# Softmax maxima and sums of a quantized cross-attention: maxima from the scores in PSUM, sums by products over transposed exponentials

## The chip, the cores and the metric

The kernel runs on one core of a Trainium2 chip. The metric is the device time of one execution in microseconds. Of the kernel before, eight runs are known: median 4922.11, from 4911.96 to 4927.17. One more execution was profiled; every duration and every instant below is from its trace, instants counted from the start of its span.

A core has five engines with a queue of instructions each: TensorE (PE, whose weight loads are shown as PEld), VectorE (DVE), ScalarE (ACT), GpSimd (POOL) and SyncE (SP, which here only issues transfers). Every engine works through its queue in order; semaphores tie them together.

## The reference, cut to what matters

The network is four blocks one after another on x (4 x 1024 tokens of 288 numbers) with a context of 4 x 64 tokens. The change is in the third block, a transformer block whose attention is "fake quantized": queries, keys and values are rounded to 256 levels over the whole tensor, and so are the probabilities, whose step is the largest probability of the whole tensor divided by 255. Its cross-attention, with 16 heads of 18 numbers:

```python
def _quant_attention(x, ctx, Wq, Wk, Wv, Wo, bo):
    q = (x @ Wq).reshape(bsz, sq, H, HD).transpose(0, 2, 1, 3)
    k = (ctx @ Wk).reshape(bsz, sk, H, HD).transpose(0, 2, 1, 3)
    v = (ctx @ Wv).reshape(bsz, sk, H, HD).transpose(0, 2, 1, 3)
    q = _fake_quant(q, NBITS)
    k = _fake_quant(k, NBITS)
    v = _fake_quant(v, NBITS)
    scale = 1.0 / np.sqrt(HD).astype(np.float32)
    scores = jnp.einsum('bhqd,bhkd->bhqk', q, k) * scale
    probs = jax.nn.softmax(scores, axis=-1)
    probs = _fake_quant(probs, SMBITS, always_zero=True)
    out = jnp.einsum('bhqk,bhkd->bhqd', probs, v)
```

Since the step of the probabilities is known only when the largest of all of them is, the kernel goes over the scores twice. The **first pass** finds, for every token and head, the largest exponential and the sum of the 64 exponentials; the largest quotient of the two over the tensor gives the step. The **second pass** computes the exponentials again, rounds them to levels and multiplies them by the values.

## The kernel before, in words

The function is `fq_tail`. Its first half, under `with (self.psum8("f2"), ...)` in line 3274, is the first pass; the rest is the second pass together with the block's feed-forward stage. P is 128, H 16 heads, T 64 context tokens, NG 4 groups of four heads, HP 32 (a head's 18 numbers padded to 32), and NT 32 tiles of 128 tokens, eight for each of the four samples b.

For each of the 32 tiles t the first pass does this:

- **Rounding** on VectorE: two operations in `fq_levels` (L818, L819) and a third (L3302) turn the tile's queries `qn` into integer levels, written in bf16 to one of three padded tiles `pads`.
- **Transposes** on TensorE (L3308, four of 128x128 into one PSUM bank), copied by ScalarE to `qT` (L3312) and written by a transfer of SP to a scratch tensor `qb` (L3313), from which the second pass reads.
- **Scores** on TensorE (L3318): four products, one for each group of heads, with `qT` as the weights and 256 columns of `kbd4` (four heads by 64 keys, block diagonal), into two PSUM banks. Tokens are on the partitions, head and key along the row.
- **Exponentials** on ScalarE (L3325), two of 128x512, into `e` (f32). The scale is read from a register, `rstep`.
- **Maxima** on VectorE (L3331): the largest of the 64 exponentials of each head, to `top`.
- **Sums** of the 64: two halvings by additions on GpSimd (L3333, 512 a row, and L3335, 256 a row), and the last 16 on VectorE (L3336), to `sums`.

PSUM is eight buffers of one bank (`psum8`), used in turn. The work tiles have three buffers each.

Behind the loop stands `prob_shift` (L2475), a chain mostly on VectorE over all 32 x 16 values of a partition: the reciprocal of the sums (L2483), its product with `top`, the largest over all partitions (L825 and a reduction over partitions on GpSimd), a logarithm (L838), and three bf16 `parts` (L2493). When it is done, the pools of the first pass are given back, and SP issues the feed-forward weights (`w`, L2517) and then the first `qT` of the second pass (L3362).

The order of the instructions in the queues is not that of the source: a scheduler in the language's compiler moves them within the dependencies, such as the roundings of later tiles ahead of the maxima of earlier ones. The function that prepares the next block's weights, `self_aside`, is spread through the stage as well; its reductions over weights (L1581 and L1582, on VectorE) stand among the last tiles of the first pass.

Of the kernel before, what the change touches and what calls it, by code (L numbers as in the profile page):

```python
# [28 lines left out]
F32 = mybir.dt.float32  # L29
BF16 = mybir.dt.bfloat16  # L30
I32 = mybir.dt.int32
AF = mybir.ActivationFunctionType
ALU = mybir.AluOpType
AX = mybir.AxisListType
PSUM = bass.MemoryType.PSUM

P = 128
B, S, C, H, D, T, FF = 4, 1024, 288, 16, 18, 64, 1152
NTB = S // P
NT = B * NTB  # L40
CK, NC3 = 96, 3
HP = 32
NG = 4
# [1136 lines left out]
class Fast(Net):  # L1180
# [2080 lines left out]
    def fq_tail(self, w, kq, keep, rawq, mx, nmn, beside):  # L3261
# [4 lines left out]
        tc, nc = self.tc, self.nc  # L3266
        with ExitStack() as es:
# [4 lines left out]
            kt = {k: gp.tile(keep[k][1], BF16, name=k) for k in ("kbd", "vbd")}  # L3272
            qb = [dr.tile([P, NG, S], BF16, name=f"qb{b}") for b in range(B)]
            with (
                self.psum8("f2"),
                tc.tile_pool(name="f2q", bufs=1) as qp,
                self.work("f2k0", 3),
            ):
                kt["kbd4"] = qp.tile(keep["kbd4"][1], BF16, name="kbd4")
                for k, (d, _) in keep.items():  # L3280
                    nc.sync.dma_start(kt[k], d)
                top = qp.tile([P, NT, H], F32, name="top")
                sums = qp.tile([P, NT, H], F32, name="sums")
                qn = qp.tile([P, NT, C], F32, name="qn")
                for b in range(B):
                    nc.sync.dma_start(qn[:, b * NTB : (b + 1) * NTB, :], rawq[b])
                pads = [qp.tile([P, H, HP], BF16, name=f"pads{n}") for n in range(3)]
                for pd in pads:
                    nc.gpsimd.memset(pd, 0.0)
                q = self.global_params(gp, mx, nmn, "qq")  # L3290
                self.watch_range(-0.5, 255.5, q["zp"], "qzext")
                step = gp.tile([P, 1], F32, name="step")
                nc.vector.tensor_scalar(
                    step, q["d"], kq["d"][:, 0:1], SCALE, ALU.mult, ALU.mult
                )
                rstep = self.scale_register("cstep", step)

                for t in range(NT):
                    b, j = divmod(t, NTB)
                    pd = pads[t % 3]  # L3300
                    self.fq_levels(qn[:, t, :], q, 0)
                    nc.vector.tensor_scalar(  # L3302
                        pd[:, :, :D], self.heads(qn[:, t, :]), q["top"], None, ALU.min
                    )
                    ps = self.ps1(BF16)
                    pf = pd.rearrange("p h d -> p (h d)")
                    for g in range(NG):
                        nc.tensor.transpose(  # L3308
                            ps[:, g * P : (g + 1) * P], pf[:, g * P : (g + 1) * P], self.idb
                        )  # L3310
                    qT = self.wk.tile([P, NG, P], BF16, tag="qT1", name="qT1")
                    nc.scalar.copy(qT, ps[:, : NG * P].rearrange("p (g t) -> p g t", t=P))  # L3312
                    nc.sync.dma_start(qb[b][:, :, j * P : (j + 1) * P], qT)  # L3313
                    e = self.wk.tile([P, H, T], F32, tag="e1", name="e1")
                    for m in range(2):
                        ps = self.ps1()
                        for g in (2 * m, 2 * m + 1):
                            nc.tensor.matmul(  # L3318
                                ps[:, (g % 2) * 256 : (g % 2 + 1) * 256],
                                lhsT=qT[:, g, :],  # L3320
                                rhs=kt["kbd4"][:, b, g, :],
                                start=True,
                                stop=True,
                            )
                        nc.scalar.activation(  # L3325
                            e[:, 8 * m : 8 * m + 8, :],
                            ps.rearrange("p (h k) -> p h k", k=T),
                            AF.Exp,
                            scale=rstep,
                        )  # L3330
                    nc.vector.tensor_reduce(top[:, t, :], e, AX.X, ALU.max)  # L3331
                    e2 = self.wk.tile([P, H, T // 2], F32, tag="e2", name="e2")
                    nc.gpsimd.tensor_tensor(e2, e[:, :, : T // 2], e[:, :, T // 2 :], ALU.add)  # L3333
                    e4 = self.wk.tile([P, H, T // 4], F32, tag="e4", name="e4")
                    nc.gpsimd.tensor_tensor(e4, e2[:, :, : T // 4], e2[:, :, T // 4 :], ALU.add)  # L3335
                    nc.vector.tensor_reduce(sums[:, t, :], e4, AX.X, ALU.add)  # L3336
                pd, parts = self.prob_shift(gp, qp, top, sums, step)
            pv = gp.tile([P, 1], F32, name="pv")
            nc.vector.tensor_tensor(pv, pd, kq["d"][:, 1:2], ALU.mult)
# [304 lines left out]
```

## Time and profile before

| what | us |
|---|---|
| median of eight runs | 4922.11 |
| the profiled execution, its time | 4919.14 |
| its span, first to last instruction | 4917.3 |
| busy in the span: PE, PEld | 4237.8, 1704.6 |
| busy in the span: DVE, ACT, POOL | 3004.4, 3067.5, 1263.3 |
| mean granted TensorE clock (1 is full) | 0.853 |
| first pass over the context, first rounding to last sum | 2936.0 to 3041.7 |
| `prob_shift`, to its last part | 3041.7 to 3058.4 |
| `w` and the first `qT` landing, first addition of the second pass | 3077.9 |

The profiled execution lies 3.0 us below the median of the runs. In a line of groups the columns are: source line, engine, operation, output and input by the program's names with their shapes and the number of instructions; then their busy time in us and the mean duration in ns; then the idle time of the engine just before them and what ended it. In a line of the timeline: start in us, duration in us, engine, line, operation. A duration is longer than the distance to the next start where instructions of one engine overlap. In a line by stretches: the stretch, its length, the busy time of each engine with the number of its instructions, the mean granted TensorE clock, the share of the transfer engines and GB/s.

### The profile page before, as it was taken

The numbers are of one execution on the slowest core, as the hardware profiler recorded it, in microseconds if no ns is written. First come the engines' busy times: TensorE is split into PE (matmuls) and PEld (weight loads), VectorE is DVE, ScalarE is ACT, GpSimd is POOL, SyncE is SP. The second block draws the span as 40 slices with busy tenths as digits, with TensorE's granted clock in tenths as the row PEclk, the third lists the DMA queues.
The fourth block names the chain that finished last, engine by engine and source line by source line (L and its number), as shares of the span: only waits on it lengthen the run. The fifth ranks groups of instructions, "written<-read, shape, count | busy, mean of one in ns | idle before, by whom it ended". The sixth has DMA issues, their size and how long they took to land. (4 is left out here: it accounts for less than half of the span.)

```text
span 4917.3 us, 63638 instructions
## 1 busy us (share of the span) xinstructions
PE 4237.8 (86%) x23227; PEld 1704.6 (35%) x23227; DVE 3004.4 (61%) x6707; ACT 3067.5 (62%) x4347; POOL 1263.3 (26%) x1900
## 2 busy tenths in 40 slices
PE   4999998888998979998788863899998999998776
PEld 2223223445565411110233331455443223222343
DVE  8355445755654589999788878333234355445775
ACT  3776775664753279998888853212113776775796
POOL 2001001543222576410112225111111001003664
PEclk9999999889999955555788885899998999998897
DMA  3000002100001221000010022101000000001000
GB/s 85 3 5 21 14 8 74 41 31 7 13 13 55 112 63 33 26 7 0 22 28 25 23 93 70 32 9 34 1 3 17 2 4 29 7 12 38 12 17 21
DMA packets 137700, 135.98 MB, mean 28 GB/s; under 512 B 69276, under 2 KB 114972, under 8 KB 135712
## 3 DMA queue, kind: packets, MB, share of 16 engines
q1 hardware_dynamic: 136176, 128.13, 8.6%
q0 software_dynamic: 1200, 3.69, 0.3%
q8 instruction: 184, 3.01, 0.3%
q14 instruction: 140, 1.15, 0.1%
HBM read 79.92 MB, written 43.47 MB: 25 GB/s over the span
## 5 line engine op out<-in xcount | busy, mean ns | idle before, releaser
L2082 ACT ACTIVATE e<-ps 128x1024 f32<-128x1024 f32 x1024 | 992.6, 1021 | 406.9 <-PE ps L2072 399.5
L2072 PE MATMUL ps<-qT,kT 32*128 32x512 f32 x4096 | 622.4, 647 | 2.0 <-DVE sext L1994 2.0
L3110 DVE TENSOR_REDUCE top<-e 128x2 f32<-128x2048 f32 x256 | 563.6, 2280 | 14.8 <-ACT e L3103 14.6
L2028 PE MATMUL ps<-e,v 128*32 128x512 f32 x4096 | 555.0, 613 | 8.5 <-DVE oT L2039 8.5
L3479 PE MATMUL ps<-qk 32*128 32x512 bf16 x1024 | 499.9, 604 | 40.7 <-ACT e L3103 38.8
L3528 ACT ACTIVATE e<-ps 128x1024 f32<-128x1024 f32 x512 | 484.0, 1053 | 76.8 <-PE ps L3519 59.2
L3103 ACT ACTIVATE e<-ps 128x1024 f32<-128x1024 f32 x512 | 520.5, 1153 | 6.8 <-PE ps L3479 3.7
L1807 POOL TENSOR_TENSOR x<-x,y 128x288 f32<-128x288 f32 x192 | 153.5, 808 | 787.8 <-DVE y L1806 482.2
L3531 DVE TENSOR_SCALAR eb<-e 128x2048 bf16<-128x2048 f32 x256 | 322.0, 1261 | 47.1 <-ACT e L3528 44.6
L3519 PE MATMUL ps<-qk,kz 64*128 64x512 bf16 x1024 | 224.6, 436 | 48.0 <-ACT e L3528 46.2
L2546 PE MATMUL psf<-hT,w 128*128 128x512 f32 x576 | 257.9, 600 | 0.6 <-ACT hT L2538 0.6
L2072 PEld LDWEIGHTS ps<-qT,kT 32*128 32x128 f32 x4096 | 183.6, 184 | 201.0 <-issue 127.7
L1427 POOL TENSOR_TENSOR h<-h,g 128x288 f32<-128x288 f32 x160 | 130.8, 819 | 426.0 <-ACT h L1424 416.1
L2028 PEld LDWEIGHTS ps<-e,v 128*32 128x32 f32 x4096 | 81.3, 108 | 403.1 <-issue 344.4
L3479 PEld LDWEIGHTS <-qk 32*128 32x128 bf16 x1024 | 53.0, 99 | 465.1 <-issue 464.2
L3428 ACT ACTIVATE gl<-psf,bf 128x512 f32<-128x512 f32 x72 | 46.0, 684 | 269.5 <-PE psf L2550 265.1
L1356 ACT COPY qT<-ps 128x640 bf16<-128x640 bf16 (+3 forms) x252 | 149.7, 640 | 76.8 <-PE ps L1351 76.6
L1924 POOL TENSOR_TENSOR v<-y,wv1b 128x288 f32<-128x288 f32 x64 | 51.7, 814 | 559.1 <-DVE y L1921 559.1
L1351 PE MATMUL ps<-idb,q 128*128 128x128 bf16 (+2 forms) x1128 | 110.7, 243 | 91.1 <-ACT q L1335 60.9
L3432 DVE SCALAR_TENSOR_TENSOR u<-psf,bf,gl 128x512 f32<-128x512 f32 x72 | 51.2, 746 | 218.5 <-ACT gl L3428 218.5
L278 PEld LDWEIGHTS <-qT 98*128 98x128 bf16 (+2 forms) x1344 | 135.5, 105 | 120.8 <-issue 49.3
L3103 ACT ACTIVATION_READ_ACCUMULATOR e<-ps 128x1 f32 x512 | 172.9, 338 | 0.0
(509 smaller groups left out, 7755.4 us busy)
## 6 DMA issues: line engine op xcount, KB each, us to landing
raw<-y SPq DMA_DIRECT2D x32, 432.0 KB
in<-raw SPq DMA_DIRECT2D x30, 432.0 KB
kz<-qk SPq DMA_DIRECT2D x128, 64.0 KB
wn<-in_L_wfc SPq DMA_DIRECT2D x12, 432.0 KB
x<-in_x SPq DMA_DIRECT2D x4, 1152.0 KB
vvo<-vt SPq DMA_DIRECT2D x16, 288.0 KB
vo<-vvo SPq DMA_DIRECT2D x4, 1152.0 KB
rawq<-y SPq DMA_DIRECT2D x32, 144.0 KB
```

Source lines behind the costliest of these rows:

```text
L1356: nc.scalar.copy(qT[:, c0 : c0 + r, j0 * P : (j0 + per) * P].rearrange("p c (a t) -> p a c t", a=per), ps[:width, : per * r * P].rearrange ...
L1807: nc.gpsimd.tensor_tensor(self.x[:, t, :], self.x[:, t, :], y, ALU.add)
L2028: nc.tensor.matmul(acc[i * HP : (i + 1) * HP, :], lhsT=st["v"][:, kt, h * (D + 1) : h * (D + 1) + HP], rhs=es_[i // 2][:, i % 2, :], start ...
L2072: nc.tensor.matmul(pss[i // 2][:, i % 2, :], lhsT=self.row_tile(kT, i)[:, kt * P : (kt + 1) * P], rhs=self.row_tile(qT, i)[:, qh * 512 : ( ...
L2082: nc.scalar.activation(e, ps, AF.Exp, scale=SCALE)
L2546: nc.tensor.matmul(o, lhsT=lhs(i)[:, c, :], rhs=rhs(i)[:, c, :], start=(c == 0), stop=False)
L3103: nc.scalar.activation(e[:, j, :].rearrange("p (a n) -> p a n", a=2), sc, AF.Exp, scale=rstep, accum_out=sums[:, t, h0 + j : h0 + j + 1],)
L3110: nc.vector.tensor_reduce(top[:, t, h0 : h0 + 2], e, AX.X, ALU.max)
L3479: self.last = self.nc.tensor.matmul(ps[:, c, :], lhsT=self.row_tile(qT, i)[:, g, qt * P : (qt + 1) * P], rhs=self.row_tile(kT, i)[:, g, c ...
L3519: nc.tensor.matmul(pss[i][:, n, :], lhsT=kz[rows, i, kt * P : (kt + 1) * P], rhs=qT[rows, g, qh * 512 : (qh + 1) * 512], start=True, stop= ...
L3528: nc.scalar.activation(e[:, 2 * n : 2 * n + 2, :], ps, AF.Exp, scale=step)
L3531: nc.vector.tensor_scalar(eb, e, MAGIC, MAGIC, ALU.add, ALU.subtract)
```

## The change

The first pass is written anew for four tiles at a time (a set; there are eight).

For each tile, `largest` does the rounding, the transposes, the copy to `qT` (now a part of a 512-token tile for the set) and the four score products as before. The scores go to one buffer of two PSUM banks, and VectorE takes the maximum of the scores straight from PSUM. The exponential of all the maxima is taken once, after the loop (`top`, 128x512).

For each set, `total` computes the scores a second time the other way round, with keys on the partitions and 512 tokens along the row: for each group of heads a pair of 64-row bf16 products (`kbd`) into two banks, and one exponential of 128x1024 into `e`. Then eight f32 products with `pick`, a matrix of zeros and ones, add up the 64 rows of each head; each gives 32 rows of one bank, `acc`, so that four of them fill it, and the second four add to the first. ScalarE copies `acc` to `sT`, four small f32 products with `back` (16 columns) turn it back to tokens on the partitions, and VectorE copies 128x64 of it to `sums`.

`total` is a generator with a step after each exponential, one after `sT` and its end; a step of each running `total` is taken after each `largest`. So the sums of a set are worked out among the next two sets' tiles, and those of the last set after the loop.

PSUM goes from eight buffers of one bank to three of two banks (`ps2`) and two of one (`ps1`). The additions on GpSimd are gone.

```diff
-                self.psum8("f2"),
+                self.psum_attn("f2"),
...
-                for t in range(NT):
+                pick = qp.tile([P, 2, HP], F32, name="pick")
+                nc.gpsimd.memset(pick, 0.0)
+                for k in range(4):
+                    rows = slice(k % 2 * 64, (k % 2 + 1) * 64)
+                    nc.gpsimd.memset(pick[rows, k // 2, k : k + 1], 1.0)
+                back = qp.tile([P, H], F32, name="back")
+                nc.gpsimd.tensor_copy(
+                    back.rearrange("p (g i) -> p g i", i=4),
+                    self.idf.rearrange("p (g k) -> p g k", k=HP)[:, :, :4],
+                )
+
+                def largest(t, qT):
...
-                    qT = self.wk.tile([P, NG, P], BF16, tag="qT1", name="qT1")
                     nc.scalar.copy(qT, ps[:, : NG * P].rearrange("p (g t) -> p g t", t=P))
                     nc.sync.dma_start(qb[b][:, :, j * P : (j + 1) * P], qT)
-                    e = self.wk.tile([P, H, T], F32, tag="e1", name="e1")
-                    for m in range(2):
-                        ps = self.ps1()
-                        for g in (2 * m, 2 * m + 1):
+                    ps = self.ps2()
+                    for g in range(NG):
+                        nc.tensor.matmul(
+                            ps[:, g // 2, g % 2 * 256 : (g % 2 + 1) * 256],
+                            lhsT=qT[:, g, :],
+                            rhs=kt["kbd4"][:, b, g, :],
+                            start=True,
+                            stop=True,
+                        )
+                    nc.vector.tensor_reduce(
+                        top[:, t, :], ps.rearrange("p a (h k) -> p (a h) k", k=T), AX.X, ALU.max
+                    )
+
+                def total(n, qT):
+
+                    es_ = []
+                    for g in range(NG):
+                        ps = self.ps2()
+                        for pr in range(2):
+                            rows = slice(pr * 64, (pr + 1) * 64)
                             nc.tensor.matmul(
-                                ps[:, (g % 2) * 256 : (g % 2 + 1) * 256],
-                                lhsT=qT[:, g, :],
-                                rhs=kt["kbd4"][:, b, g, :],
-                                start=True,
-                                stop=True,
+                                ps[:, pr, :], lhsT=kt["kbd"][rows, n // 2, g, :],
+                                rhs=qT[rows, g, :], start=True, stop=True,
                             )
-                        nc.scalar.activation(
-                            e[:, 8 * m : 8 * m + 8, :],
-                            ps.rearrange("p (h k) -> p h k", k=T),
-                            AF.Exp,
-                            scale=rstep,
+                        e = self.wk.tile([P, 2, 512], F32, tag="e1", name="e1", bufs=6)
+                        nc.scalar.activation(e, ps, AF.Exp, scale=rstep)
+                        es_.append(e)
+                        yield
+                    acc = self.ps1()
+                    for pr in range(2):
+                        for g in range(NG):
+                            nc.tensor.matmul(
+                                acc[g * HP : (g + 1) * HP, :], lhsT=pick[:, pr, :],
+                                rhs=es_[g][:, pr, :], start=(pr == 0), stop=(pr == 1),
+                            )
+                    sT = self.wk.tile([P, 512], F32, tag="sT", name="sT")
+                    nc.scalar.copy(sT, acc)
+                    yield
+                    ps = self.ps1()
+                    for j in range(4):
+                        nc.tensor.matmul(
+                            ps[:, j * H : (j + 1) * H], lhsT=sT[:, j * P : (j + 1) * P],
+                            rhs=back, start=True, stop=True,
                         )
-                    nc.vector.tensor_reduce(top[:, t, :], e, AX.X, ALU.max)
-                    e2 = self.wk.tile([P, H, T // 2], F32, tag="e2", name="e2")
-                    nc.gpsimd.tensor_tensor(e2, e[:, :, : T // 2], e[:, :, T // 2 :], ALU.add)
-                    e4 = self.wk.tile([P, H, T // 4], F32, tag="e4", name="e4")
-                    nc.gpsimd.tensor_tensor(e4, e2[:, :, : T // 4], e2[:, :, T // 4 :], ALU.add)
-                    nc.vector.tensor_reduce(sums[:, t, :], e4, AX.X, ALU.add)
+                    nc.vector.tensor_copy(
+                        sums[:, 4 * n : 4 * n + 4, :].rearrange("p t h -> p (t h)"),
+                        ps[:, : 4 * H],
+                    )
+
+                running = []
+                for n in range(NT // 4):
+                    qT = self.wk.tile([P, NG, 512], BF16, tag="qT1", name="qT1")
+                    for j in range(4):
+                        largest(4 * n + j, qT[:, :, j * P : (j + 1) * P])
+                        running = [t for t in running if next(t, running) is not running]
+                    running.append(total(n, qT))
+                while running:
+                    running = [t for t in running if next(t, running) is not running]
+                nc.scalar.activation(top, top, AF.Exp, scale=rstep)
                 pd, parts = self.prob_shift(gp, qp, top, sums, step)
```

## The prediction

> **What bounds it now.** The chain of waits is no help: it holds one 0.8 us step, since it follows a branch at the end of the kernel. So I read the granted clock and the engines by stretches, then the groups of the stretch that the change touches, then its timeline. The stretches, columns PE, PEld, DVE, ACT and POOL busy, PEclk, DMA share, GB/s:
>
> ```profile
> 2350.00:2363.00 13.00, 8.62 (x68) 3.21 (x67) 9.49 (x10) 12.64 (x15) 1.39 (x2) 1.00 0.09 21
> 2364.00:2370.00 6.00, 5.38 (x27) 0.97 (x25) 4.55 (x4) 5.98 (x8) 0.00 (x0) 0.50 0.00 0
> 2936.00:3041.70 105.70, 49.66 (x256) 27.57 (x256) 95.14 (x178) 53.05 (x97) 64.34 (x64) 0.50 0.26 66
> 3041.70:3058.50 16.80, 0.00 (x0) 0.00 (x0) 16.37 (x50) 2.54 (x3) 0.38 (x1) 0.50 0.01 1
> ```
>
> The third line is the first pass over the context: 105.7 us, DVE busy for 95, no other engine for 65, the clock at half throughout. The fourth is the chain on DVE behind it (`prob_shift`), which starts once all sums are there. So the pass is DVE's, and what it loses is read from its groups:
>
> ```profile
> L3333 POOL TENSOR_TENSOR e<-e 128x512 f32<-128x512 f32 x32 | 40.5, 1267 | 39.2 <-ACT e L3325 30.4 <-ACT qT L3312 8.5
> L3331 DVE TENSOR_REDUCE top<-e 128x16 f32<-128x1024 f32 x32 | 38.7, 1208 | 3.1 <-ACT e L3325 3.0
> L819 DVE TENSOR_SCALAR qn<-qn,qqnzp 128x288 f32<-128x288 f32 x32 | 19.1, 598 | 0.0
> L818 DVE TENSOR_SCALAR qn<-qn,qqrd 128x288 f32<-128x288 f32 x32 | 15.6, 497 | 0.0
> L3336 DVE TENSOR_REDUCE sums<-e 128x16 f32<-128x256 f32 x32 | 13.0, 408 | 7.5 <-POOL e L3335 7.5
> ```
>
> L819 takes 598 ns in the mean, but its median is 365. The timeline shows why:
>
> ```profile
> 2984.81 1.26 POOL L3333 TENSOR_TENSOR e<-e 128x512 f32<-128x512 f32 x1 [0.25 <-ACT e L3325]
> 2984.94 1.30 DVE L819 TENSOR_SCALAR qn<-qn,qqnzp 128x288 f32<-128x288 f32 x1
> 2986.15 0.73 POOL L3335 TENSOR_TENSOR e<-e 128x256 f32<-128x256 f32 x1
> 2986.16 0.89 DVE L818 TENSOR_SCALAR qn<-qn,qqrd 128x288 f32<-128x288 f32 x1
> 2986.97 1.21 DVE L3331 TENSOR_REDUCE top<-e 128x16 f32<-128x1024 f32 x1
> 2988.10 0.40 DVE L3336 TENSOR_REDUCE sums<-e 128x16 f32<-128x256 f32 x1
> ```
>
> A rounding on DVE that starts inside a POOL addition ends with it, whatever its own 0.36 us; the reduction does not mind (1.21). From L3302 at 2979.72 to L3302 at 2998.58 six tiles pass, 3.14 us each. Of that, start to start, the maximum is 1.13, the sum 0.33, three roundings 3 x 0.28 = 0.84; the other 0.84 is DVE held behind POOL or waiting.
>
> **What the change removes and adds on DVE.** Gone are 32 sums (0.33), all POOL work (64.5 us) and with it the 0.84. Kept are the roundings, 0.84, and the maximum, now over two PSUM banks. No row reduces from PSUM. The nearest pair: a 128x512 reduction from SBUF takes 686 ns (L1219), a 128x512 copy out of PSUM 690 (L3395), so I take 1.13; bounds 1.13 and 1.20. [...] New is one copy of 128x64 out of PSUM for four tiles, about 0.16 (64 elements at the reduction's 1.1 ns, and 0.09). A set of four tiles thus costs DVE 4 x (0.84 + 1.13) + 0.16 = 8.04 us, where it took 12.56.
>
> **On ACT**, a set: four qT copies (589 ns, 0.54 start to start), four exponentials of 128x1024 (1.02, as L3103), one copy of the sums' 128x512 (0.59): 6.9 us, against 4 x (0.54 + 1.08) = 6.5. Under DVE's 8.04, so only its order matters.
>
> **On PE**, a set had 16 transposes and 16 products of 256 columns (0.63 and 1.03 us per four at half clock). Added: (S) four pairs of 64-row bf16 products; a pair lies side by side (two L3376 start 0.1 us apart, the third 0.4 later, at half clock), so 0.43 a pair at half, 0.21 at full clock. (P) eight f32 products, 32 columns each, over the exponentials: four of L2028 take 0.64 us and eight 1.06 at full clock, so 0.43 for four, 0.85 at half. (B) four small f32 products whose weight loads set the pace: L2546's load is 0.19, up to 0.337 at half; 0.9 and 1.5 us together. Sum with what was there: about 5 us a set at full clock, 10 at half. POOL's new memsets and copy stand early in its order, beside the block before. SP issues the same 32 qb writes, from a tile of a set; each still waits only for its ACT copy.
>
> **The new waits.** In the built order the eight are not together: P's first five wait on PE for the exponentials of groups 2 and 3, then come the four score products (K) of the next set's first tile, then P's last three. Behind P on PE stands K, and for K waits DVE's next maximum. ACT's copy sT waits for P (behind it: the next exponential and two qT copies); B waits on PE for sT (behind it a transpose and K); DVE's copy of the sums waits for B, and behind it stand the roundings. And an S may start only when the maximum of the tile before has freed its two banks.
>
> I walked one set by these orders, 0 being the end of a sums copy. Full clock: maxima at 1.35 (waits 0.2 for K), 2.5, 3.9; third S at 3.65, its exponential 4.1 to 5.1, qT copy to 5.65, K done 6.3; roundings end at 7.0, first maximum to 8.1; P ends 6.75, sT 7.4, B 8.4, sums 8.6. So **8.6 us** a set, DVE idle 0.5. Half clock: the last maximum of the set starts at 4.5 and the exponentials end at 5.9; K is done at 7.85, P 8.7, sT 9.35, B 10.95: **11.15 us**, and PE's loop is the bound.
>
> **The clock** thus decides. The pass now keeps half clock with 53% busy PE (49.66 of 94 us). In the first two lines above the neighbour stage does what I expect here: at full clock with 13 us of which PE is truly fed some 35% (three lots of 0.21 in 1.83 us) it falls to half at 2363.4, with no gap over 0.53 us; at half clock PE is packed, and after 6 us it is back. Its mean over 2345 to 2900 is 0.84. After the change PE is fed 5/8.6 = 58% at full and 90% at half: above both. I take 0.84, 68% of the time at full: 1/(0.68/8.6 + 0.32/11.15) = **9.3 us** a set. [...]
>
> **The sum.** First maximum at 2940.2 as K allows; maxima and roundings of set 0, nothing overlapped yet, bring the first maximum of set 1 to 2947.9. Set 1 has S but no B: 9.0, still cold, to 2956.9. Five sets at 9.3 bring that of set 7 to 3003.4. Then the tail, which the old pass had not: three maxima with two of the 1.34 us weight reductions between them end after 7.9; the exponentials of the last set stand on ACT behind the exponential of the maxima (0.63) and sT, and end at 12.2; P, sT, B, sums at 15.2 (full) or 18 (half); 16 taken. The reciprocal L2483 starts at 3003.4 + 16 = 3019.4; it started at 3041.8. **22.4 us** saved. The 5.4 us of weight reductions that stood between the old sums are inside the tail. Behind: the chain of 16.8 us is unchanged but for two roundings of 0.28 that move ahead of it (left out), and the loads that the next stage waits for (w, then qT, landing 3078) are issued by SP when `parts` L2493 frees the pools, so they move along.
>
> The profiled execution took 4919.1, 3.0 below the median 4922.1. 4919.1 - 22.4 = 4896.7; put beside the median, **4900**.
>
> **The rivals**, with reciprocal = 2956.9 + 5p + tail:
> - Full clock throughout: p 8.6, tail 15.2, 3015.1, saved 26.7: 4895. For: 58% fed. Against: the neighbour's falls.
> - Half clock throughout: p 11.15, tail 18, 3030.7, saved 11.1: 4911. For: 0.50 in all of the old pass, whose transposes and K alone are 0.43 + 0.85 of 3.14 us. Against: 90% packed at half; the neighbour rose on less than that.
> - Slower: half clock, and P's eight lie one behind another, because five wait singly and K cuts them: 8 x 0.85 = 6.8 in place of 1.7, p 16.2, tail 23, 3060.9, a loss of 19: 4941. It decides from p = 13.8 on. Against: L2028 overlaps by column groups, and only groups 2 and 3 wait.
> - The pass shortens and the next stage waits anyway for its loads: 4922. Against: SP waited 12.9 us for `parts` ahead of them.
> - The eight issued really together would spare the second drain after K, 0.4 us a set: inside the first two cases.
>
> **Numbers.** Forecast 0.52, full clock 0.22, half clock 0.14, loads 0.06, slower 0.06. The range takes in the full-clock case with no DVE wait at all (p 8.04: 2.8 less, 4892) and the half-clock case (4911), and 2 us each way for the PSUM price and the measurement: 4890 to 4914. A measurement here tells about 0.2% (9.8 us) from no change; the half-clock case lies on that edge and is halved: faster 0.81, same 0.13, slower 0.06.
>
> **What would show it.** In the profile after: L819 and L818 means near 365 ns; maxima from `ps` near 1.21 us; first maxima of sets 9.3 us apart; PEclk over 0.8 between 2957 and 3010; L2483 near 3019; `parts` to the first rounding of the next stage as long as before. Wrong if maxima of 1.5 us or more, P groups of over 2 us, a clock of 0.50, or sets over 13.8 us.

## The result, and the profile after

The changed kernel takes 4908.77 us (median of 11 runs, 4900.96 to 4917.37), the kernel before 4922.73 beside it (31 runs, 4911.96 to 4931.23): a ratio of 0.9972, 95% interval [0.9964, 0.998]. It is 14 us faster, where 22 were forecast; 4908.8 lies inside the forecast range of 4890 to 4914. The profiled execution has a span of 4903.3 us (4917.3 before).

Below, "the stage" is the first pass over the context, from its first rounding (L818) to the reciprocal of the sums (L2483), and "a set" the distance between the first maxima of two sets of four tiles. The stage took 2936.02 to 3041.76 us before, 105.7 us, and 2940.91 to 3030.40 after, 89.5 us: **16.2 us shorter**, where 22.4 were worked out. Its groups on VectorE, columns as before:

```profile
L3334 DVE TENSOR_REDUCE top<-ps 128x16 f32<-128x1024 f32 x32 | 38.3, 1219 | 2.8 <-PE ps L3327 2.8
L3314 DVE TENSOR_SCALAR pads<-qn,qqtop 128x288 bf16<-128x288 f32 x32 | 11.7, 365 | 0.0
L819 DVE TENSOR_SCALAR qn<-qn,qqnzp 128x288 f32<-128x288 f32 x32 | 11.6, 363 | 0.0
L3369 DVE COPY sums<-ps 128x64 f32<-128x64 f32 x8 | 1.8, 225 | 12.2 <-PE ps L3365 12.2
```

L819 fell from 598 to 363 ns, since no addition on GpSimd holds it any more, and the maximum from PSUM takes 1.219 us where the one from SBUF took 1.208. That much came as forecast. New is the idle time in the last line: VectorE waits 12.2 us in all for the sums to come back from TensorE (L3365). The stretches of the stage, columns as in the prediction (PE, PEld, DVE, ACT, POOL busy, PEclk, DMA share, GB/s):

```profile
2945.00:2950.00 5.00, 2.92 (x21) 1.99 (x19) 4.68 (x5) 1.07 (x2) 0.00 (x0) 0.77 0.90 225
2955.00:2960.00 5.00, 4.32 (x20) 2.03 (x20) 3.73 (x7) 3.45 (x6) 0.00 (x0) 0.50 0.30 81
2965.00:3010.00 45.00, 40.73 (x304) 19.86 (x301) 37.60 (x78) 32.24 (x45) 0.00 (x0) 1.00 0.23 57
```

From 2965 us on TensorE has the full clock without a break, and it is busy for 40.7 of 45 us, more than VectorE with 37.6. Five sets there take 9.61 us each. One of them in the timeline (lines of other instructions left out):

```profile
2999.50 1.97 PE L3356 MATMUL ps<-e,pick 128*32 128x512 f32 x10
...
3001.40 0.61 PE L3327 MATMUL ps<-kbd,qT 128*128 128x256 bf16 x4
...
3001.94 1.06 PE L3356 MATMUL ps<-e,pick 128*32 128x512 f32 x6
3002.07 1.22 DVE L3334 TENSOR_REDUCE top<-ps 128x16 f32<-128x1024 f32 x1
...
3002.94 0.39 PE L3345 MATMUL ps<-qT,kbd 64*128 64x512 bf16 x2
3003.06 0.59 ACT L3361 COPY sT<-ps 128x512 f32<-128x512 f32 x1 [2.22 <-PE ps L3356]
...
3003.70 1.06 PE L3365 MATMUL ps<-back,sT 128*128 128x16 f32 x8
...
3004.80 0.23 DVE L3369 COPY sums<-ps 128x64 f32<-128x64 f32 x1 [1.51 <-PE ps L3365]
```

The eight f32 products P (L3356) leave 16 records, 10 ahead of the scores K (L3327) and 6 behind: an f32 product leaves two records here (in e2 below, with bf16, there are 8 for the eight). Start to start P holds TensorE's queue for 1.90 and 1.00 us, **2.90 us a set**; the prediction had 0.85. Behind it follow the copy sT, the products back and, 1.51 us late, VectorE's copy of the sums.

### The profile page after: what moved, and what is told of

The parts are those of the page before. It is cut to its first block, busy times and chain, and to the rows that moved or that the text cites. A ratio compares the mean times of both kernels' runs of the same rounds, so it can differ in the third digit from the quotient of the medians.

```text
span 4903.3 us, 63966 instructions
## 1 busy us (share of the span) xinstructions
PE 4271.1 (87%) x23483; PEld 1710.3 (35%) x23483; DVE 2975.9 (61%) x6683; ACT 3069.8 (63%) x4324; POOL 1198.9 (24%) x1842
## 3 DMA queue, kind: packets, MB, share of 16 engines
q14 instruction: 138, 1.13, 0.1%
## 5 line engine op out<-in xcount | busy, mean ns | idle before, releaser
L3110 DVE TENSOR_REDUCE top<-e 128x2 f32<-128x2048 f32 x256 | 563.6, 2280 | 16.6 <-ACT e L3103 16.4
L2028 PE MATMUL ps<-e,v 128*32 128x512 f32 x4096 | 554.3, 612 | 8.5 <-DVE oT L2039 8.5
L3526 PE MATMUL ps<-qk 32*128 32x512 bf16 x1024 | 499.9, 604 | 40.7 <-ACT e L3103 38.9
L2028 PEld LDWEIGHTS ps<-e,v 128*32 128x32 f32 x4096 | 81.3, 108 | 402.4 <-issue 343.8
```

Source lines behind the costliest of these rows:

```text
L2028: nc.tensor.matmul(acc[i * HP : (i + 1) * HP, :], lhsT=st["v"][:, kt, h * (D + 1) : h * (D + 1) + HP], rhs=es_[i // 2][:, i % 2, :], start ...
L3110: nc.vector.tensor_reduce(top[:, t, h0 : h0 + 2], e, AX.X, ALU.max)
L3526: self.last = self.nc.tensor.matmul(ps[:, c, :], lhsT=self.row_tile(qT, i)[:, g, qt * P : (qt + 1) * P], rhs=self.row_tile(kT, i)[:, g, c ...
```

## The experiments

At first two theories stood against each other. The **chain** theory ("loop theory" in the expectations of the first runs): a set is as long as the way from the sums copy over the next maxima, the scores that wait for their PSUM buffer, the exponentials, P, sT and the products back to the next sums copy. The **TensorE** theory ("PE theory" there): TensorE's own work, with P at 2.9 us, is what a set costs. Beside them stood the questions whether GpSimd's additions had cost what the prediction said, and what each part of the change gives alone. All runs, with the stage from each profile (there is no e8 and no e9). "A set" is the mean of the sets at the clock given; in e1 and e7, whose maxima change their order, it is the distance between two sums copies:

| run | stage, us | a set, us (clock) | median, us | ratio to before |
|---|---|---|---|---|
| before | 105.7 | 12.56 (0.50) | 4922.7 | 1 |
| changed | 89.5 | 9.61 (1.00) | 4908.8 | 0.9972 [0.9964, 0.9980] |
| changed, again | 89.6 | 9.61 (1.00) | 4907.3 | 0.9964 [0.9950, 0.9978] |
| e1 sums later | 93.7 | 10.1 (1.00) | 4906.9 | 0.9970 [0.9959, 0.9981] |
| e2 bf16 sums | 85.6 | 8.84 (1.00), 9.8 (0.82) | 4903.7 | 0.9959 [0.9946, 0.9973] |
| e6 later and bf16 | 91.8 | 9.07 (1.00), 10.15 (0.84) | 4909.3 | 0.9975 [0.9966, 0.9984] |
| e7 P in two halves | 91.8 | 9.83 (1.00) | 4906.9 | 0.9972 [0.9960, 0.9983] |
| e10 P in one block | 87.3 | 9.24 (1.00) | 4906.8 | 0.9964 [0.9950, 0.9977] |
| e11 one block and bf16 | 91.6 | 10.2 (0.84), 11.9 (0.60) | 4906.7 | 0.9973 [0.9961, 0.9985] |
| e13 own buffers | 95.5 | 9.20 (1.00) | 4911.3 | 0.9978 [0.9969, 0.9987] |
| e3 no additions | 89.9 | 11.04 (0.50) | 4910.2 | 0.9977 [0.9968, 0.9986] |
| e12 e3, more on TensorE | 83.6 | 9.28 (1.00) | 4901.9 | 0.9959 [0.9946, 0.9973] |
| e4 maxima alone | 122.3 | (0.50) | 4938.0 | 1.0036 [1.0023, 1.0050] |
| e5 P by group | 135.8 | 16.3 (1.00) | 4955.1 | 1.0069 [1.0055, 1.0083] |

The two columns agree: the stage's gain over 4922.7 gives the ratio within 0.001 in every row. The stage tells the variants apart where their times, with intervals of some 10 us, do not.

**The changed kernel once more**

> The changed kernel once more, unedited. If the 4.9 us by which its stage began later (first rounding at 2940.9 us against 2936.0) were the chance of one execution, the stage starts anywhere within 2 to 4 us of 2936 this time; if the change caused it, at 2940 or 2941 again. Inside the stage (first rounding to the reciprocal) 88 to 90 us and 9.6 us a set at full clock either way.

The stage began at 2942.8 us, and between 2937.1 and 2944.2 in all thirteen profiles taken after that of before, among them those of e3 and e4, which have the structure of before (2942.8 and 2940.2). So the changed kernel's late start is not the change's doing; the one profile of before, with 2936.0, began early. Lengths of the stage can be compared, instants less so.

**e1: the sums one tile later**

```diff
                     nc.scalar.copy(sT, acc)
-                    yield
+                    yield; yield
```

> The products that bring the sums back and the sums copy come one tile later. Loop theory: the 1.5 us a set that VectorE waits at the sums copy go, a set takes 8.1 to 8.5 us at full clock (its own work is 8.04), the stage 80 to 82 us in place of 89, the time some 4901 us (0.9956 to 0.996 of the kernel before). PE theory: PE sets the 9.6 us, a set stays at 9.4 or more and the time at 4907 to 4909 us (0.997).

The chain theory's numbers did not come. The other theory's bound holds (9.4 us or more, 4907 us), but it did not say that a set would become longer, and it did: the wait at the sums copy is gone and a set takes 10.1 us. The waits between 2962 and 3013 us (who waited for whom: us in total, times, longest), of the changed kernel and then of e1:

```profile
DVE sums L3369 <- PE ps L3365: 7.6, 5, 1.5
...
PE ps L3345 <- DVE top L3334: 1.7, 5, 0.3
PE ps L3320 <- DVE sums L3369: 1.6, 5, 0.3
...
PE ps L3327 <- ACT qT L3323: 0.7, 4, 0.2
```

```profile
DVE top L3334 <- PE ps L3327: 6.8, 11, 1.1
PE ps L3327 <- ACT qT L3323: 6.7, 9, 1.2
```

VectorE waits nearly as long as before, now at its maxima, for the scores K; and TensorE waits for the `qT` copies that K needs. These copies stand on ScalarE behind the copy sT, which waits for P: 11.8 us in the same stretch, 2.8 the longest. So the chain theory falls in the form in which it named the sums copy, and in e1 the waits point to a chain over ScalarE rather than to TensorE's work, which fills 37.5 of the 45 us from 2965 to 3010. In the changed kernel ScalarE waits for P as well (13.4 us in all), but TensorE waits only 0.7 for `qT`. The first fence gives TensorE's side: it waited 1.7 + 1.6 + 0.7 = 4.0 us in 5.3 sets, 0.75 a set, so that its own work is about 8.9 of the 9.61 us.

**e2: transposed exponentials and ones in bf16**

```diff
-                pick = qp.tile([P, 2, HP], F32, name="pick")
+                pick = qp.tile([P, 2, HP], BF16, name="pick")
...
-                        e = self.wk.tile([P, 2, 512], F32, tag="e1", name="e1", bufs=6)
+                        e = self.wk.tile([P, 2, 512], BF16, tag="e1", name="e1", bufs=6)
```

> The transposed exponentials and the ones are bf16 in place of f32, so the sums are those of exponentials rounded to bf16. If an f32 product is two matmuls, L3356 has 64 matmul records in place of 128 (8 a set in place of 16), P takes about 1.5 us a set in place of 3.0, and a set 8.1 to 8.5 us under the loop theory (1.3 to 1.5 us less waiting at the sums copy); under the PE theory 8.1 to 8.3 too. The tail is 2 to 3 us shorter. Stage 77 to 80 us, time 4897 to 4900 us (0.995). If the size of P does not matter, a set stays at 9.6 us and the time at 0.997.

P in e2, two products, one, and the last five:

```profile
2995.30 0.39 PE L3356 MATMUL ps<-e,pick 128*32 128x512 bf16 x2
...
2996.09 0.39 PE L3356 MATMUL ps<-e,pick 128*32 128x512 bf16 x1
...
2997.34 0.59 PE L3356 MATMUL ps<-e,pick 128*32 128x512 bf16 x5
```

Eight records a set and not sixteen. At full clock a set takes 8.84 us, 0.77 less than in the changed kernel, so P's size is a part of the 9.61. But for two sets (2960 to 2979 us) the mean clock was 0.82 and 0.83, and these took 9.4 and 10.2 us. The first fall, in the columns of the stretches:

```profile
2957.80:2964.50 6.70, 4.62 (x43) 2.62 (x40) 6.24 (x16) 4.89 (x8) 0.00 (x0) 1.00 0.19 40
2964.70:2967.90 3.20, 3.20 (x16) 1.45 (x14) 2.60 (x4) 1.67 (x3) 0.00 (x0) 0.50 0.42 87
```

From 2978 to 3019 us the same products a set kept the full clock, so less work on TensorE does not by itself bring the clock down; what does was not shown. Set, stage and time came out above what was expected (8.84 for 8.1 to 8.5, 85.6 for 77 to 80); the stage is the shortest of the variants that compute sums of all 64 exponentials.

**e6: both**

> Both edits: sums one tile later, and bf16 exponentials and ones (the sums are those of rounded exponentials). Loop theory: VectorE waits for nothing in the middle of the stage, a set takes its own 8.04 to 8.2 us, the tail is 2 to 3 us shorter than in the changed kernel, the stage 75 to 78 us and the time 4895 to 4897 us (0.9946). If PE sets the pace a set is 8.1 or more as well, but then the edit of the order alone gained nothing, and both together no more than bf16 alone.

The edits of e1 and e2 together, 91.8 us: 6.2 worse than bf16 alone. From 2980 us on the mean clock was 0.84 to 0.85 (a set 10.15 us; at full clock 9.07), so that the five regular sets took 2.5 us more than in e2; the other 3.7 lie behind them, from the first maximum of set 7 to the reciprocal (21.1 for 17.3). The expectation missed at full clock too, where 8.04 to 8.2 had been expected, and it left out the clock.

**e5: P by group**

```diff
-                    for pr in range(2):
-                        for g in range(NG):
+                        for pr in range(2):
                             nc.tensor.matmul(
```

(Moved into the loop over the groups, each pair behind its exponential.)

> The eight f32 products of a set are issued two at a time, behind the exponential of their group, in place of all together. If products into different columns of the array run beside each other and two into the same columns do not: a pair of records of one product took 1.04 us alone in the tail of the changed kernel, so four groups of two products take 4 x 2.1 = 8.3 us a set in place of 3.0, PE has 11.3 us of work a set in place of 6.1, a set takes 11.3 to 12.5 us, the stage 100 to 110 us, and the time 4920 to 4930 us (0.9996 to 1.0016). If only the length of the chain behind the last exponential matters: P's share behind it falls from 2.7 to 2.1 us or less, a set takes 8.8 to 9.4 us, and the time is 4902 to 4906 us (0.996).

The direction is the first theory's, and its size was too small: a set takes 16.3 us. A tile of it:

```profile
2981.30 1.02 ACT L3350 ACTIVATE e<-ps 128x1024 f32<-128x1024 f32 x1 [2.45 <-PE ps L3345]
...
2982.38 1.91 PE L3353 MATMUL ps<-e,pick 128*32 128x512 f32 x4 [0.85 <-ACT e L3350]
...
2984.22 0.61 PE L3327 MATMUL ps<-kbd,qT 128*128 128x256 bf16 x4
```

Two f32 products into the same columns take 1.84 us until K may start, and TensorE first waits 0.85 for the exponential with all else behind it in its queue. So "issued together" is worth 46 us of stage.

**e7: P in two halves**

```diff
                     for pr in range(2):
+                        if pr: yield
                         for g in range(NG):
```

> The changed kernel with the second four f32 products of a set issued one tile after the first four. Run e1 showed that taking the wait away at the sums copy moves it to the maxima, so something else sets the 9.6 us. If it is P as one block of 3 us in TensorE's queue, ahead of the transposes and scores that VectorE's next maxima need: a set takes 8.8 to 9.3 us at full clock, the stage 84 to 87 us in place of 89.5, the time 4903 to 4906 us (0.9965). If it is the one-bank PSUM buffers, of which the accumulator now holds one of two for a tile longer: the transposes wait, a set takes 10 us or more, the stage 92 us or more, and the time 4911 us or more (0.998).

A set takes 9.83 us and the stage 91.8, by neither theory's number. The scheduler made four pieces of P:

```profile
2982.64 1.04 PE L3357 MATMUL ps<-e,pick 128*32 128x512 f32 x2
...
2984.48 1.05 PE L3357 MATMUL ps<-e,pick 128*32 128x512 f32 x4
...
2986.06 1.04 PE L3357 MATMUL ps<-e,pick 128*32 128x512 f32 x2
...
2987.20 1.07 PE L3357 MATMUL ps<-e,pick 128*32 128x512 f32 x8
```

This is the price list of the study: one f32 product (2 records) takes 1.04 us, two into different columns 1.05, four 1.07. P costs by rounds over the column groups, not by products. There are four rounds instead of three, and TensorE is busy for 9.68 of 10 us (2990 to 3000).

**e10: P in one block**

```diff
-                    for pr in range(2):
+                    with tc.issue_after(self.lastk):
+                      for pr in range(2):
```

(`lastk` is the last score product of the tile; the block keeps P's products behind it.)

> The changed kernel with its eight f32 products of a set really in one block in TensorE's queue, behind the scores of the tile: in the changed kernel they stand five, scores of a tile, three (10 records in 1.97 us and 6 in 1.06), so that the four column groups are filled in three rounds, where two would do. TensorE theory: its queue sets the 9.61 us a set, a round of 0.86 to 1.06 us falls away, L3356's 16 records take 1.9 to 2.0 us together, a set takes 8.5 to 8.8 us, the stage (first rounding to the reciprocal) 82 to 85 us in place of 89.5, the time 4901 to 4903 us (0.996). Chain theory (sums copy to maxima to scores to exponentials to products to sums copy): the block starts 2.4 us later and ends 0.9 us later than now, a set takes 10 us or more, the stage 92 us or more and the time 4911 us (0.998).

```profile
2988.34 1.02 ACT L3351 ACTIVATE e<-ps 128x1024 f32<-128x1024 f32 x1 [0.26 <-PE ps L3346]
2988.71 2.61 PE L3358 MATMUL ps<-e,pick 128*32 128x512 f32 x16
```

All 16 records stand together and still take 2.61 us: the first three products run while the last exponential is on ScalarE (to 2989.36), and two full rounds follow it. P holds the queue for 2.54 us here (to the next scores at 2991.25), and for 2.32 to 2.54, 2.43 in the mean, in the five regular sets, in place of 2.90. So about 0.47 us a set is spared on TensorE, and the sets, 8.83 to 9.47 us long, take 9.24 in the mean, 0.37 less. Both numbers missed, since only half of a round fell away, but the direction is the TensorE theory's, and the chain theory's sign missed too: the block starts 5.1 us behind the sums copy, where P started 4.3 behind it, and no set became longer for it.

**e11: one block and bf16**

> The same block, and transposed exponentials and ones in bf16 (the sums are those of rounded exponentials): L3356's 8 records take some 0.6 us. TensorE theory: TensorE has 1.3 us less a set than with the block alone, VectorE's own 8.04 us becomes the bound, a set takes 8.1 to 8.4 us at full clock, the stage 77 to 80 us, the time 4896 to 4899 us (0.995). Chain theory: between bf16 alone and the block alone, a set 8.8 to 9.2, stage 85 to 87 us.

The edits of e10 and e2 together. Missed: TensorE was busy for 7.5 of 10 us, the mean clock was 0.84, and a set took 10.2 us; the last of the five took 11.9 at a clock of 0.60. As in e6, the smaller P came with a lower clock than in the changed kernel.

**e13: buffers of their own for the transposed scores**

```diff
-                self.psum_attn("f2"),
+                self.tc.tile_pool(name="f2s", bufs=2, space=PSUM) as self.pa, self.tc.tile_pool(name="f2b", bufs=4, space=PSUM) as self.pb,
...
-                        ps = self.ps2()
                         for pr in range(2):
+                            ps = self.ps1()
...
-                        nc.scalar.activation(e, ps, AF.Exp, scale=rstep)
+                            nc.scalar.activation(e[:, pr, :], ps, AF.Exp, scale=rstep)
```

> The changed kernel with the transposed scores in one-bank PSUM buffers (four of them, with the transposes, the accumulator and the returned sums; each exponential in two halves of 128x512) and two two-bank buffers left to the scores that VectorE takes the maxima of, in place of three that both kinds of scores share. Chain theory (a group's transposed scores wait until a maximum has freed a shared buffer, and the exponential, P, the products back and the sums copy hang on it, in VectorE's order in front of the next maxima): the scores no longer wait for L3334, the wait at the sums copy falls from 1.5 us a set to 0.5 or less, a set takes 8.6 to 9.1 us at full clock, the stage 81 to 85 us in place of 89.5, the time 4900 to 4903 us (0.9958). If TensorE's queue with P's three rounds sets the pace by itself: a set stays at 9.4 to 9.7 us and VectorE waits as long as before, at whatever instruction, the stage is 88 to 91 us and the time 4907 us (0.997).

The transposed scores no longer wait for a maximum, and a set takes 9.20 us on average; the wait at the sums copy stayed at 1.4 to 1.5. The stretches of the middle show what bounds it:

```profile
2980.00:2990.00 10.00, 9.67 (x69) 4.26 (x66) 8.46 (x19) 7.38 (x16) 0.00 (x0) 1.00 0.23 57
2990.00:3000.00 10.00, 9.62 (x74) 4.75 (x72) 8.59 (x17) 7.38 (x16) 0.00 (x0) 1.00 0.25 63
```

TensorE hardly rests, with VectorE idle for 1.5 of 10 us. Its work is then some 9 us a set, as the TensorE theory has it, and 0.4 us of the 9.61 went with the edit. That the shared buffers cost them is likely but not shown apart, since the edit also halves the exponentials. The set's 9.20 lies between the two ranges expected, and the stage lies outside both. From the first maximum of set 2 to that of set 7 it took 48.05 us, as long as the changed kernel's 48.1, because the first of these sets, with the clock at 0.91, took 11.3. The 6 us that the stage lost lie behind: from the first maximum of set 7 to the reciprocal 24.8 us passed in place of 18.7, with the clock at 0.50 from 3022 to 3028 us.

**e3: the kernel before without GpSimd's additions**

```diff
...
-                    nc.gpsimd.tensor_tensor(e2, e[:, :, : T // 2], e[:, :, T // 2 :], ALU.add)
...
-                    nc.gpsimd.tensor_tensor(e4, e2[:, :, : T // 4], e2[:, :, T // 4 :], ALU.add)
-                    nc.vector.tensor_reduce(sums[:, t, :], e4, AX.X, ALU.add)
+                    nc.vector.tensor_reduce(sums[:, t, :], e[:, :, : T // 4], AX.X, ALU.add)
```

> The kernel before without its two GpSimd additions a tile; VectorE's sum goes over the first 16 of each 64 exponentials only, so the sums leave out three quarters and VectorE's own work stays what it was. If the additions slow VectorE down (the 0.84 us a tile of the prediction): the three roundings fall from 598, 497 and 442 ns to 360 to 370, a tile takes 2.3 us in place of 3.14, the stage (first rounding to the reciprocal) 78 to 82 us in place of 105.8 and the time some 4898 us (0.995). If VectorE waits for something else: durations and stage stay, 4920 us (0.9995).

The sums leave out three quarters of the exponentials, so this run measures and is no kernel to use. The roundings fell to 361 to 364 ns, as the first theory says, and the stage to 89.9 us: the additions alone had cost 15.8 us, nearly as much as the whole change brought. The shorter roundings make up some 14 of it: the three of a tile took 1.54 us together and take 1.09, in 32 tiles. It did not fall to 80, because now VectorE waits for ScalarE, and ScalarE for scores at half clock:

```profile
L3331 DVE TENSOR_REDUCE top<-e 128x16 f32<-128x1024 f32 x32 | 39.0, 1220 | 10.7 <-ACT e L3325 10.5
```

**e12: e3 with more work on TensorE**

```diff
+                    ps = self.ps1()
+                    for k in range(6):
+                        nc.tensor.matmul(
+                            ps[:, k % 2 * 256 : (k % 2 + 1) * 256], lhsT=qT[:, k % 4, :],
+                            rhs=kt["kbd4"][:, b, k % 4, :], start=True, stop=True,
+                        )
```

> Run e3 (the kernel before without GpSimd's additions, sums over a quarter of the exponentials) with six more score products a tile that nothing reads, so that TensorE has 1.9 us a tile at full clock and 3.2 at half. Run e3 had the clock at 0.50 from 2960 to 3020 us, the changed kernel at 1.00, and its stage was 89.9 us. If the granted clock follows TensorE's load: it rises to 0.8 to 1.0 in the stage, the scores of a tile take 0.61 us in place of 1.03, and the stage is 78 to 84 us although TensorE has more to do. If the clock is set by something else and stays at 0.50: TensorE needs 3.2 us a tile and the stage is 103 us or more, the time 4920 us or more.

The first theory, with 83.6 us inside its range. The same stretch in e3 and then in e12:

```profile
2960.00:3010.00 50.00, 28.24 (x148) 16.09 (x148) 43.84 (x94) 28.93 (x56) 0.00 (x0) 0.50 0.21 48
```

```profile
2960.00:3010.00 50.00, 33.52 (x306) 25.32 (x303) 48.60 (x104) 36.19 (x65) 0.00 (x0) 1.00 0.26 59
```

Six useless products a tile raise TensorE from 148 to 306 records and its clock from 0.50 to 1.00. Four score products then take 0.61 us in place of 1.03, VectorE is busy for 48.6 of 50 us, and the stage is 6.4 us shorter. The medians follow (4910.2 and 4901.9), though their intervals just overlap. The two runs agree with a clock that rises with TensorE's load: e3, with TensorE busy for 56% of the 50 us and waits of up to 2.7 us between its products, had the clock at 0.50 in every stretch read from 2945 to 3020 us; in e12, busy for 67%, it was 1.00. But load alone does not describe e2, where TensorE was busy for 69% of the 6.7 us before the fall at 2964.6 us, and rested for 2.1 us of them in all.

**e4: maxima from PSUM alone**

```diff
-                self.psum8("f2"),
+                self.psum_attn("f2"),
...
-                    nc.vector.tensor_reduce(top[:, t, :], e, AX.X, ALU.max)
+                    nc.vector.tensor_reduce(
+                        top[:, t, :], ps.rearrange("p a (h k) -> p (a h) k", k=T), AX.X, ALU.max
+                    )
```

(With one exponential of 128x1024 behind the maximum, and that of the maxima after the loop; GpSimd's additions stay.)

> The kernel before with the maxima from PSUM alone (one exponential of 128x1024 behind it, the sums as before on GpSimd and VectorE). By the prediction's sum the gain of the change is the GpSimd additions that go, so here nothing is gained: the roundings stay near 598, 497 and 442 ns, the maximum takes 1.21 us in place of 1.13, the stage 105 to 109 us, the time 4920 to 4925 us (0.9995 to 1.0006). If the order maximum, exponential, sum is what costs (VectorE waiting for ScalarE): the stage falls to 100 us or less and the time to 4916 (0.9988).

Worse than both: 122.3 us. Groups between 2945 and 3055 us:

```profile
L3324 DVE TENSOR_REDUCE top<-ps 128x16 f32<-128x1024 f32 x31 | 37.7, 1218 | 8.9 <-PE ps L3317 8.9
L818 DVE TENSOR_SCALAR qn<-qn,qqrd 128x288 f32<-128x288 f32 x27 | 23.0, 853 | 0.0
...
L3334 DVE TENSOR_REDUCE sums<-e 128x16 f32<-128x256 f32 x30 | 12.3, 410 | 6.1 <-POOL e L3333 6.1
```

The maxima cost what they cost in the changed kernel. But GpSimd's additions now meet the roundings more often (L818 853 ns, 497 before), and VectorE waits for scores and for sums, 15.0 us together, where it waited 10.6 before. How much of this is the order and how much the smaller number of PSUM buffers was not tried apart. So the maxima from PSUM are no gain of their own; they pay only with the sums gone from GpSimd.

## Why the prediction was right, and where it was not

**What bounded the kernel: right.** VectorE, held by GpSimd's additions: e3 shows it alone, with the roundings at 363 ns and 15.8 us of stage.

**VectorE's work: right.** 8.04 us a set were worked out; the maximum came at 1.219 us (1.208 from SBUF), the roundings at 0.36, and VectorE is busy for 37.6 of 45 us, 8.0 of 9.61. No run shows where the upper bound of 1.20 for the maximum, or the price of PSUM that the forecast's range allows for, would come from: two maxima back to back take 2.36 us (at 2945.09 and 2947.77), so that one takes 1.14 start to start, for the 1.13 of the sum. Only the sums copy was put too low, 0.16 for 0.225.

**TensorE's work: wrong, and this is the step that failed.** "About 5 us a set at full clock" was 8.9. The largest part is the term P, "0.43 for four": the row L2028 was read as one record to a product. Its eight records in 1.06 us are four products, as e7's price list shows, so that a round of four costs 0.88 (the distance of two products into the same columns in e5) to 1.06 and not 0.43, and the built order, five and three, makes three rounds: 2.90 us for the 0.85 of the sum. The rest was too small as well, start to start and without waits: transposes and K 3.43 us a set (2.6 by the prediction's 0.43 + 0.85 a tile at half clock), S 1.36 (0.84), B 1.06 (0.9). With P at that size TensorE, not VectorE, is the fuller engine, and 8.6 at full clock became 9.61: a set grows and shrinks with P, from 8.84 (e2) over 9.24 (e10) and 9.83 (e7) to 16.3 (e5). The prediction had named P groups of over 2 us as a sign of being wrong: in the regular sets P stands in two groups, of 1.90 and 1.00 us, which pass that test one by one and fail it together.

**The clock: wrong the other way.** A mean of 0.84 was taken; from 2965 us on it was 1.00 in all of the regular sets. That the clock would decide was right: e12 shows it, with 83.6 us of stage at 1.00 where e3 has 89.9 at 0.50. The two errors offset each other: 9.3 was forecast for a set and 9.61 came, so that the two lie so close is in part luck. The longer P may also be a reason why the clock stayed up: e2, e6 and e11, with a shorter P, had a mean clock of 0.82 to 0.85 in a part of the stage; but e2 kept the full clock in another part, so this is not shown.

**The sum, from the first rounding on.** First maximum after 4.18 us, as forecast. First maximum of set 2 after 22.7 (20.9 forecast: two sets at mostly half clock). Five sets 48.1 (46.5). Tail 18.7 (16): there three products of set 6's P stand alone, at 1.04 us each, and P of set 7 takes 3.34. Together 1.8 + 1.6 + 2.7 = 6.1 us, which is the difference between 22.4 and the 16.2 measured.

**Behind the stage: right.** From the reciprocal to the end of the span 1875.6 us passed before, 1872.9 and 1875.6 in the two profiles of the changed kernel, and from the last `parts` to the first addition of the next stage 19.3 us, 19.5 before: the loads moved along, and the gain arrived whole.

**The rivals.** Full clock throughout came as far as the clock goes, but with it a set took 9.61 us and not 8.6. Half clock throughout would have given 4911, near the time measured, but the profile excludes it, with the clock at 1.00 from 2965 us on. P unpacked was priced at 16.2 us a set; e5 built it and took 16.3, 4955 us. That the eight really together would spare 0.4 us a set came nearly true: e10 spared 0.37 in the mean of five sets.

**What stays open.** Which wait closes the last 0.7 us between TensorE's 8.9 and 9.61 was not settled: e1 moved VectorE's wait without removing it, e13 removed one wait of TensorE and won 0.4, and no variant with f32 sums came under 9.2 in the mean. ScalarE's copy sT, which waits 2.2 us a set for P with the exponential and the `qT` copies behind it, is a candidate that no run took away. What sets the granted clock between these variants is open too. No version tried was clearly faster than the changed kernel; e2 (0.9959) and e10 (0.9964) overlap with it.

## What to carry to other kernels

Before work is moved to another engine, count that engine's queue start to start, with the number of records that one product leaves in the trace (here two in f32, one in bf16), since a row of means does not say what a product is. A stage that is short of TensorE work can pay for its low clock elsewhere, as e3 (0.50, 89.9 us) and e12 (1.00, 83.6 us) show: look at the granted clock of the stretch before giving or taking work. And take a two-part change apart on the chip: here the part that gave the gain (additions off GpSimd) brought 15.8 us of stage, while the other alone cost 16.6.

## What the runs showed of the hardware that was not expected

- Adding matmuls whose result nobody reads made a stage 6.4 us shorter, with the granted clock at 1.00 in place of 0.50 (e12 against e3).
- One, two and four f32 products of 128x512 into different column groups take 1.04, 1.05 and 1.07 us; two into the same columns 1.91 (e7, e5). In bf16 a lone one takes 0.39 and five 0.59 (e2).
- VectorE's maximum over 1024 numbers a row took 1.219 us from two PSUM banks and 1.208 to 1.220 from SBUF (the kernel before, e3).
- The clock fell to 0.50 for some 3 us in e2 behind 6.7 us in which TensorE was busy for 4.6 and rested for 2.1 in all.
